# A four-layer graph attention kernel: what is loaded first, and when the later layers' weights and the second batch's adjacency follow

## The chip, the cores and the metric

The kernel runs on one core of one Trainium2 chip. The core has a matrix engine (PE; its weight loads are listed as PEld), a vector engine (DVE), a scalar engine (ACT), a general engine (POOL, GpSimd), a queue engine (SP), and 16 DMA engines [...]. The metric is the device time of one execution in microseconds (us), as the median of repeated runs. Before the change it is 3160.04 us (3 runs, 3157.3 to 3164.76).

## What is computed

16 graphs ("batches") of 1024 nodes with 256 features each, and one 1024 x 1024 adjacency of 0 and 1 per graph. Four attention layers follow one another; each normalizes the features, clamps them at zero, attends over the neighbours and adds the result to the features. Cut to what matters:

```python
# x: (16, 1024, 256) float32, adj: (16, 1024, 1024) int32
h = maximum(layernorm(x), 0); x = x + L0(h, adj, W, a)   # softmax over neighbours of leaky_relu(f1_i + f2_j)
h = maximum(layernorm(x), 0); x = x + L1(h, adj, W, a)   # exp(-leaky_relu(...)), then elu
h = maximum(layernorm(x), 0); x = x + L2(h, adj, W, a)   # softmax of relu(...), then elu
h = maximum(layernorm(x), 0); x = x + L3(h, adj, ...)    # 4 heads of 64, leaky_relu 0.01, bias, relu, layernorm
# each of L0, L1, L2:
#   Wh = h @ W;  e_ij = act(Wh_i @ a[:256] + Wh_j @ a[256:]);  e_ij masked by adj
#   out_i = sum_j softmax_j(e_ij) Wh_j
```

## The kernel before

The kernel is written as Python generators that are traced into one program. Two streams of batches (even ones and odd ones) are interleaved; each `yield t` advances its stream's counter by `t`, and the stream whose counter is lower is traced next. The order of tracing is the program order. A scheduler then places each engine's instructions by that order, but lets an instruction that it takes to be ready early float ahead; `tc.keep_in_program_order(i)` pins `i` behind whatever was traced before it on the same engine.

The loads of one batch, and the test of its adjacency (which looks for values other than 0 and 1):

```python
    def load(b):
        narrow = narrows[b % 2]                       # adjacency as bytes, in DRAM
        ...
        for c in range(NI // 2):                      # NI = 8: four casts int32 -> uint8, DRAM to DRAM
            cast = nc.gpsimd.dma_start(rows[c], adj[b, ts(c, 2 * P), :]...)
            tc.keep_in_program_order(cast)
        yield
        mask = masks[b] = nodes.tile([P, NI // 2, N, 2], U8, name="mask")
        for c in range(NI // 2):                      # four transposing loads
            turn = nc.sync.dma_start_transpose(mask[:, c]..., narrow[:, ts(c, P)])
            if b > 1:
                tc.keep_in_program_order(turn)
            yield
        xs[b] = nodes.tile([P, NI, D], F32, name="x_b")
        queue = nc.gpsimd if b > 1 else nc.sync
        queue.dma_start(xs[b]..., in_blocks(x[b]))    # 1 MB of features
        yield

    def test(b):
        for i in range(NI):
            adj_i = adjs.tile([P, N], BF, name="adj_i")          # 4 buffers
            nc.gpsimd.dma_start(adj_i, adj[b, ts(i, P), :])
            square = nc.scalar.activation(adj_i, adj_i, AF.Square, ..., accum_out=squares[:, b, i : i + 1])
            tc.keep_in_program_order(square)
            yield
```

`prepare()` loads the layers' weights `W[l]` and vectors `a`, and makes from them a few extra columns of each `W[l]` (W times a), so that a projection gives the attention scores too:

```python
    def prepare():
        ...
        scratch = [edges.tile([P, N], F32, name="weights0") for _ in EXT]
        def extend(l): ...                            # 3 small DVE multiplies into W[l][:, :, D:]
        def fetch(l): ...                             # on SP: W[l], a; for l = 3 also bias, gamma, beta
        fetch(0)
        for l in range(3):
            if l == 0:
                yield
            fetch(l + 1)
            for k in range(NK):
                for s in range(2):
                    nc.vector.tensor_tensor_reduce(prod, W[l][:, k, :D], scratch[l][:, ts(s, D)], ...)   # L200
            extend(l)
            yield
        for s in range(2):
            for k in range(NK):
                nc.vector.tensor_mul(prod, W[3][:, k, :D], scratch[3][:, ts(s, D)])                      # L209
                nc.vector.tensor_reduce(wa[:, k, 3:, s], ...)                                            # L210
        extend(3)
        ...                                           # norms of the columns, by PE and DVE, into a flag
        yield
```

One batch projects its features for layer 0 (four pairs of node blocks), and then attends in each layer. `weigh` makes the eight 128 x 1024 tiles of edge weights on DVE (L292) from a row of scores in PSUM, of which there is one for both streams; while they come, the products of the first two node blocks run (L380); then those of the other six, and behind each pair of blocks the projection for the next layer (L271):

```python
        def attend(l, V, finish, then):
            behind = weigh(b, ...)
            yield from start(behind, b)
            ...
            for j in range(NI):
                next(behind)                          # DVE: weights of block j
                product(0, j)                         # PE
                product(1, j)
                yield 0.9
            for i in range(NI):
                if i > 1:
                    for j in range(NI): product(i, j)
                finish(i, accs.pop(i))                # frees the accumulator, adds into x_b
                if l == 2:
                    next(testing)
                if i != 0:
                    yield 3.6
                if i % 2 == 1:
                    yield from steps
                    steps = project(b, then, xb, i // 2, following[1])    # yields 0.5, 1.0, 2.5
                yield from islice(steps, 1)
            yield 1.0
            yield from steps
        ...
        if b == 0:
            for _ in chain(preparing, loading):       # all other weights, columns and loads of batch 0
                pass
        V = yield from attend(0, V, finish0, 1)
        next(coming, None)                            # coming = load(b + 2): its casts
        V = yield from attend(1, V, finish, 2)
        V3 = yield from attend(2, V, finish, 3)
        # then layer 3, four heads in eight half-heads of 8 x 0.9 + 0.5 + 0.5, the rest of `coming` among them
```

And the two streams:

```python
    LAG = 120.0
    def stream(first):
        if first:
            for _ in load(first):
                yield 2.0
        for b in range(first, B, 2):
            yield from batch(b)

    loading, preparing = load(0), prepare()
    for _ in islice(loading, 2 + NI // 2):
        pass
    next(preparing)
    streams = [[0.0, stream(0)], [LAG, stream(1)]]
```

## Time and profile before

| | before |
|---|---|
| time, median of 3 | 3160.04 us |
| span of the profiled execution | 3156.4 us |
| PE busy | 3003.8 us (95%) |
| DVE busy | 2376.8 us (75%) |
| POOL busy | 1078.1 us (34%) |
| ACT busy | 729.5 us (23%) |
| PE busy in the first 40 us | 17.6 us |
| PE busy from 400 to 3000 us | 2529.8 us of 2600 |
| PE busy from 3000 us to the end | 113.4 us of 156 |

A page of the profile has the busy time of each engine, the span in slices, the chain of waits that ended last, and groups of instructions by line of the kernel. A line of the timeline reads: start, duration, engine, source line, operation, what it writes and reads, how many; in brackets, how long the engine stood idle ahead of it and what ended that. In a table of windows, each row is a stretch of time with the busy time and, in brackets, the number of instructions of each engine, then the granted clock of PE (1.00 is full), the mean busy share of the 16 DMA engines (overlapping packets can bring it over 1) and the rate in GB/s.

### The profile page before, as it was taken

How to read it: one execution, taken by the hardware profiler on the slowest of the kernel's cores; microseconds unless marked ns; L12 is line 12 of the kernel's file. 1: busy time of each engine (PE TensorE's matmuls, PEld its weight loads, DVE VectorE, ACT ScalarE, POOL GpSimd, SP SyncE). 2: the span in 40 equal slices, each digit the busy share in tenths (PEclk: the TensorE clock that was granted, in tenths of full speed). 3: DMA queues.
4: the chain of work that ended last, by engine and by line, in shares of the span. 5: the costliest groups of instructions: out<-in, count | busy, mean ns of one | idle time of the engine just before them, and what ended most of it. 6: DMA issues, size and time to landing. Idle time of an engine off the chain costs nothing.

```text
span 3156.4 us, 35596 instructions
## 1 busy us (share of the span) xinstructions
PE 3003.8 (95%) x12678; PEld 2065.5 (65%) x12678; DVE 2376.8 (75%) x5243; ACT 729.5 (23%) x1729; POOL 1078.1 (34%) x1396
## 2 busy tenths in 40 slices
PE   7899999999999999999999999999999999999986
PEld 5675766668666686666767567575776757766652
DVE  5677778786878768887687876878768787787756
ACT  1221223123131221312213122131222213222130
POOL 1323325233252432423325233342324333243232
PEclk9999999999999999999999999999999999999998
DMA  5512212022120221302302122022121121001010
GB/s 112 62 19 27 47 21 50 18 27 53 15 60 7 54 30 11 67 1 54 41 8 60 14 47 34 14 54 27 40 27 22 46 27 44 11 14 27 1 27 15
DMA packets 116872, 105.53 MB, mean 33 GB/s; under 512 B 73680, under 2 KB 91216, under 8 KB 116688
## 3 DMA queue, kind: packets, MB, share of 16 engines
q0 software_dynamic: 44256, 81.80, 15.9%
q1 hardware_dynamic: 72432, 21.37, 3.6%
q8 instruction: 103, 1.69, 0.2%
q14 instruction: 81, 0.66, 0.1%
HBM read 153.49 MB, written 33.55 MB: 59 GB/s over the span
## 4 chain that ended last, share of the span: by engine, by line
PE 67%; DVE 21%; POOL 6%; ACT 2%; issue 2%; DMA 1%; ACTq 0%; SPq 0%; POOLq 0%; DVEq 0%
PE acc L380 32%; PE acc L487 19%; PE acc L271 11%; DVE weights L292 9%; PE misc L264 2%; POOL rstd L239 2%; DVE stats L251 2%; PE row L288 2%; DVE above L317 1%; DVE centered L256 1%; POOL y L447 1%; DVE above L318 1%; ACT below L315 1%; POOL x_b L319 1%; DVE y L448 1%
## 5 line engine op out<-in xcount | busy, mean ns | idle before, releaser
L380 PE MATMUL acc<-V,weights 128*128 128x257 f32 x6144 | 1439.9, 384 | 24.1 <-DVE weights L292 11.0
L380 PEld LDWEIGHTS acc<-V,weights 128*128 128x128 f32 x6144 | 1148.0, 191 | 336.0 <-DVE weights L292 83.8
L487 PE MATMUL acc<-weights,V 128*65 128x512 f32 x2048 | 960.1, 592 | 2.0 <-DVE weights L292 1.7
L292 DVE SCALAR_TENSOR_TENSOR weights<-row,ex,mask 128x1024 f32<-128x1024 f32 x512 | 626.7, 1274 | 12.6 <-PE row L288 9.1
L271 PE MATMUL acc<-W,hT 128*128 128x259 f32 (+1 forms) x2048 | 532.7, 399 | 55.5 <-DVE above L317 24.5
L239 POOL TENSOR_TENSOR rstd<-rstd,minus_half 128x2 f32<-128x2 f32 (+1 forms) x320 | 302.7, 949 | 701.9 <-DVE rstd L238 687.2
L271 PEld LDWEIGHTS acc<-W,hT 128*128 128x128 f32 x2048 | 386.3, 195 | 192.4 <-issue 68.9
L292 DVE SCALAR_TENSOR_TENSOR weights<-row,V,mask 128x1024 f32<-128x1024 f32 x384 | 475.5, 1273 | 46.9 <-PE row L288 46.9
L487 PEld LDWEIGHTS acc<-weights,V 128*65 128x65 f32 x2048 | 272.3, 138 | 351.3 <-issue 307.4
L319 POOL TENSOR_TENSOR x_b<-x_b,above 128x256 f32<-128x256 f32 x256 | 193.4, 758 | 687.8 <-DVE above L318 621.9
L315 ACT ACTIVATE below<-acc,inv 128x256 f32<-128x256 f32 x256 | 120.7, 474 | 827.6 <-DVE inv L308 532.6
L251 DVE BATCH_NORM_STATS2 stats<-x_b 128x6 f32<-128x256 f32 x512 | 208.5, 415 | 110.2 <-POOL x_b L319 102.0
L266 ACT COPY hT<-misc 128x512 f32<-128x512 f32 x256 | 149.3, 584 | 442.7 <-PE misc L264 442.5
L447 POOL TENSOR_TENSOR y<-y,bias 128x512 f32<-128x512 f32 x64 | 82.0, 1281 | 388.9 <-DVE y L505 345.2
L256 DVE TENSOR_SCALAR centered<-x_b,mv 128x256 f32<-128x256 f32 x512 | 209.4, 411 | 4.7
L264 PEld LDWEIGHTS misc<-ident,centered 128*128 128x128 f32 x1024 | 127.2, 142 | 110.0 <-issue 44.8
L264 PE MATMUL misc<-ident,centered 128*128 128x128 f32 x1024 | 164.6, 277 | 36.3 <-DVE centered L256 27.7
L333 ACT ACTIVATE V<-acc,rstd 128x3 f32<-128x3 f32 x384 | 98.9, 262 | 417.5 <-PE acc L271 416.6
L337 DVE TENSOR_SCALAR V<-acc,rstd,V 128x256 f32<-128x256 f32 x256 | 133.1, 538 | 67.0 <-ACT V L333 65.5
L317 DVE TENSOR_SCALAR above<-acc,inv 128x256 f32<-128x256 f32 x256 | 122.2, 480 | 68.0 <-ACT below L315 66.9
L497 ACT COPY sums<-acc 65x512 f32<-65x512 f32 x128 | 74.4, 581 | 353.2 <-PE acc L487 353.1
L132 ACT ACTIVATE adj_i<-adj_i,minus_half 128x1024 bf16<-128x1024 bf16 x128 | 145.8, 1139 | 0.0
(68 smaller groups left out, 1890.5 us busy)
## 6 DMA issues: line engine op xcount, KB each, us to landing
adj_i<-in_adj_dram POOLq DMA_DIRECT2D x128, 256.0 KB, 3.9
narrow<-in_adj_dram POOLq DMA_DIRECT2D x64, 256.0 KB, 9.0
out_dram<-y POOLq DMA_DIRECT2D x32, 512.0 KB, 4.0
x_b<-in_x_dram POOLq DMA_DIRECT2D x14, 1024.0 KB, 6.7
x_b<-in_x_dram SPq DMA_DIRECT2D x2, 1024.0 KB, 7.3
mask<-narrow SPq DMA_TRANSPOSE x64, 3.8
W<-in_L_gnn_W_dram SPq DMA_DIRECT2D x3, 256.0 KB, 11.4
weights<-in_L_gnn_a_dram SPq DMA_DIRECT2D x3, 256.0 KB, 12.7
```

Source lines behind the costliest of these rows:

```text
L239: nc.gpsimd.tensor_tensor(r, r, minus_half.to_broadcast([P, n]), op=ALU.pow)
L251: nc.vector.bn_stats(stats, xb[:, 2 * pair + n, :])
L256: nc.vector.tensor_scalar(centered[:, n, :], xb[:, 2 * pair + n, :], mv[:, n, 0:1], 0.0, op0=ALU.subtract, op1=ALU.max,)
L264: nc.tensor.transpose(turned[:, k, ts(n, P)], centered[:, n, ts(k, P)], ident)
L266: nc.scalar.copy(hT, turned)
L271: nc.tensor.matmul(projected, hT[:, k, ts(n, P)], W[l][:, k, :], start=(k == 0), stop=(k == NK - 1),)
L292: nc.vector.scalar_tensor_tensor(w, r, c(j), masks[b][:, j // 2, :, j % 2], op0=op, op1=ALU.mult)
L315: nc.scalar.activation(below, acc[:, :D], AF.Exp, scale=inv)
L317: nc.vector.tensor_scalar(above, acc[:, :D], inv, 0.0, op0=ALU.mult, op1=ALU.max)
L319: nc.gpsimd.tensor_add(xi, xi, above)
L380: nc.tensor.matmul(accs[i], weights[j][:, ts(i, P)], V[:, j, : D + 1], start=(j == 0), stop=(j == NI - 1),)
L487: nc.tensor.matmul(accT, V3[:, j, h, :], weights[h * NI + j][:, ts(g, HALF)], start=(j == 0), stop=(j == NI - 1),)
```

## The change

Batch 0 is to get at first only what it needs: its casts, its features, layer 0's weights and its masks. The weights of each later layer are fetched, and its extra columns made, one layer ahead of their use and pinned there in program order; the columns are made right behind the last weights tile of the layer before, the small multiplies of `extend` for layers 1 to 3 by GpSimd instead of DVE. Batch 1's casts and features follow the columns of layer 1. The test of batch 0's adjacency no longer fetches ahead. The features of batches from 2 on are pinned in program order too. `scratch` uses the other stream's weights buffers.

```diff
--- before.py
+++ after.py
@@ -96,6 +96,13 @@
     xs, masks = {}, {}
     narrows = [dram.tile([N, N // 2], BF, name=f"narrow{n}") for n in range(2)]
 
+    def fetch_nodes(b: int):
+        xs[b] = nodes.tile([P, NI, D], F32, name="x_b")
+        queue = nc.gpsimd if b > 1 else nc.sync
+        fetch = queue.dma_start(xs[b].rearrange("p (c t) f -> p c t f", t=2), in_blocks(x[b]))
+        if b > 0:
+            tc.keep_in_program_order(fetch)
+
     def load(b: int):
 
 
@@ -106,6 +113,8 @@
                 rows[c], adj[b, ts(c, 2 * P), :].rearrange("(q t) j -> q t j", t=2)
             )
             tc.keep_in_program_order(cast)
+        if b < 2:
+            fetch_nodes(b)
         yield
 
         mask = masks[b] = nodes.tile([P, NI // 2, N, 2], U8, name="mask")
@@ -113,20 +122,20 @@
             turn = nc.sync.dma_start_transpose(
                 mask[:, c].rearrange("p n t -> p (n t)").bitcast(BF), narrow[:, ts(c, P)]
             )
-            if b > 1:
-                tc.keep_in_program_order(turn)
+            tc.keep_in_program_order(turn)
             yield
-        xs[b] = nodes.tile([P, NI, D], F32, name="x_b")
-        queue = nc.gpsimd if b > 1 else nc.sync
-        queue.dma_start(xs[b].rearrange("p (c t) f -> p c t f", t=2), in_blocks(x[b]))
-        yield
+        if b > 1:
+            fetch_nodes(b)
+            yield
 
     def test(b: int):
 
         for i in range(NI):
 
             adj_i = adjs.tile([P, N], BF, name="adj_i")
-            nc.gpsimd.dma_start(adj_i, adj[b, ts(i, P), :])
+            fetch = nc.gpsimd.dma_start(adj_i, adj[b, ts(i, P), :])
+            if b == 0:
+                tc.keep_in_program_order(fetch)
 
 
             square = nc.scalar.activation(
@@ -149,6 +158,7 @@
     beta = const.tile([P, D], F32, name="beta")
 
     def prepare():
+
 
 
         forms = [
@@ -157,62 +167,70 @@
             (0.0, 1.0, -1.0),
             (L3_SLOPE, 1 - L3_SLOPE, L3_SLOPE - 1),
         ]
-        scratch = [edges.tile([P, N], F32, name="weights0") for _ in EXT]
+        scratch = [edges.tile([P, N], F32, name="weights1") for _ in EXT]
 
         def extend(l: int):
             n = EXT[l] // 3
+            engine = nc.vector if l == 0 else nc.gpsimd
             for c, factor in enumerate(forms[l]):
-                nc.vector.tensor_scalar_mul(
+                engine.tensor_scalar_mul(
                     W[l][:, :, D + c * n : D + (c + 1) * n],
                     wa[:, :, l : l + n, 0 if c == 2 else 1],
                     factor,
                 )
 
         def fetch(l: int):
+            def begin(dst: bass.AP, src: bass.AP):
+                fetched = nc.sync.dma_start(dst, src)
+                if l > 0:
+                    tc.keep_in_program_order(fetched)
+
             if l < 3:
-                nc.sync.dma_start(
-                    W[l][:, :, :D], ins[f"L{l}_W"].rearrange("(k p) o -> p k o", p=P)
-                )
-                nc.sync.dma_start(scratch[l][:, : 2 * D], on_all_partitions(ins[f"L{l}_a"], 2 * D))
+                begin(W[l][:, :, :D], ins[f"L{l}_W"].rearrange("(k p) o -> p k o", p=P))
+                begin(scratch[l][:, : 2 * D], on_all_partitions(ins[f"L{l}_a"], 2 * D))
                 return
             for k in range(NK):
-                nc.sync.dma_start(
+                begin(
                     W[3][:, k, :D].rearrange("p (h e) -> p h e", h=H),
                     ins["L3_W"][:, ts(k, P), :].rearrange("h p e -> p h e"),
                 )
             for s, name in enumerate(("L3_a_src", "L3_a_dst")):
                 first = ins[name]
-                nc.sync.dma_start(
+                begin(
                     scratch[3][:, ts(s, D)].rearrange("p (h e) -> p h e", h=H),
                     bass.AP(tensor=first.tensor, offset=first.offset, ap=[[0, P], [T * E, H], [1, E]]),
                 )
             for t, a in ((bias, ins["L3_bias"]), (gamma, ins["L3_gamma"]), (beta, ins["L3_beta"])):
-                nc.sync.dma_start(t, on_all_partitions(a, D))
-
-        fetch(0)
+                begin(t, on_all_partitions(a, D))
+
         for l in range(3):
-            if l == 0:
-                yield
-            fetch(l + 1)
+            fetch(l)
+            yield
             for k in range(NK):
                 for s in range(2):
                     prod = work.tile([P, D], F32, name="above", bufs=2)
-                    nc.vector.tensor_tensor_reduce(
+                    made = nc.vector.tensor_tensor_reduce(
                         prod, W[l][:, k, :D], scratch[l][:, ts(s, D)], op0=ALU.mult, op1=ALU.add,
                         scale=1.0, scalar=0.0, accum_out=wa[:, k, l, s : s + 1],
                     )
+                    if l > 0:
+                        tc.keep_in_program_order(made)
             extend(l)
             yield
+        fetch(3)
+        yield
         for s in range(2):
             for k in range(NK):
                 prod = work.tile([P, D], F32, name="above", bufs=2)
-                nc.vector.tensor_mul(prod, W[3][:, k, :D], scratch[3][:, ts(s, D)])
+                tc.keep_in_program_order(
+                    nc.vector.tensor_mul(prod, W[3][:, k, :D], scratch[3][:, ts(s, D)])
+                )
                 nc.vector.tensor_reduce(
                     wa[:, k, 3:, s], prod.rearrange("p (h e) -> p h e", h=H), AX.X, ALU.add
                 )
         extend(3)
 
-        nc.vector.tensor_scalar_add(beta, beta, -2.0)
+        tc.keep_in_program_order(nc.vector.tensor_scalar_add(beta, beta, -2.0))
 
         groups = (3 + H) * 2
         wa2 = small.tile([P, NK, groups], F32, name="wa2", bufs=1)
@@ -387,6 +405,13 @@
                 next(behind)
                 product(0, j)
                 product(1, j)
+                if b == 0 and j == NI - 1:
+
+
+                    next(preparing)
+                    if l == 0:
+                        next(loading[1])
+                    next(preparing, None)
                 yield 0.9
             for _ in behind:
                 pass
@@ -427,8 +452,7 @@
         for steps in pairs:
             yield from steps
         if b == 0:
-            for _ in chain(preparing, loading):
-                pass
+            next(preparing)
         V = yield from attend(0, V, finish0, 1)
         next(coming, None)
         V = yield from attend(1, V, finish, 2)
@@ -523,16 +547,13 @@
 
 
     def stream(first: int):
-        if first:
-            for _ in load(first):
-                yield 2.0
+        for _ in loading[first]:
+            yield 2.0
         for b in range(first, B, 2):
             yield from batch(b)
 
-    loading, preparing = load(0), prepare()
-
-    for _ in islice(loading, 2 + NI // 2):
-        pass
+    loading, preparing = [load(0), load(1)], prepare()
+    next(loading[0])
     next(preparing)
     streams = [[0.0, stream(0)], [LAG, stream(1)]]
     while streams:
```

## Prediction

> **What bounds the kernel now.** I first read the page's totals: PE is busy 3003.8 of 3156.4 us, so the whole change plays in the 153 us that PE is not busy. The table of windows says where these lie: 22.4 us in the first 40 us, 70 us in the 2600 us from 400 to 3000, and 42.6 us in the last 156 us.
>
> ```profile
> 5.00:10.00 5.00, 1.09 (x4) 0.72 (x4) 1.79 (x8) 0.27 (x1) 0.97 (x2) 1.00 0.98 235
> 25.00:30.00 5.00, 2.50 (x12) 1.89 (x10) 0.00 (x0) 1.01 (x3) 0.00 (x0) 0.84 1.09 314
> 60.00:80.00 20.00, 19.43 (x96) 16.26 (x94) 9.55 (x31) 2.79 (x8) 2.44 (x4) 1.00 0.00 1
> ```
>
> The last two columns are the DMA share and GB/s: at the start the DMA engines are full and PE (the second number) is idle; 40 us later PE is full and nothing is moved. Next, the chain that ended last, in order of time, for the start:
>
> ```profile
> 1.40 6.73 DMA W<-in_L_gnn_W_dram
> 8.14 23.66 DMA weights<-in_L_gnn_a_src_dram
> 31.82 0.42 DVE above L209
> ```
>
> The end waits for a vector of layer 3 that nothing needs before 150 us. The timeline shows how it gets there: SP hands it out and is held for 10 us by the full DMA engines, the masks of batch 0 stand behind it on SP, and DVE has the product with it (L209) ahead of the last V blocks of batch 0.
>
> ```profile
> 8.14 10.13 SPq L185 DMA_DIRECT2D weights<-in_L_gnn_a_src_dram  x1
> 29.32 10.36 SPq L113 DMA_TRANSPOSE mask<-narrow  x4
> 31.82 0.42 DVE L209 TENSOR_TENSOR above<-W,weights 128x256 f32<-128x256 f32 x1 [7.55 <-DMA weights<-in_L_gnn_a_src_dram]
> 38.28 1.28 DVE L292 SCALAR_TENSOR_TENSOR weights<-row,V,mask 128x1024 f32<-128x1024 f32 x1
> ```
>
> So the first weights tile starts at 38.28 us. Last, the later windows: one stream runs alone until about 146 us and again from about 3000 us. Alone, the end of a layer leaves PE without work; with two streams a little is lost where a batch begins:
>
> ```profile
> 3005.07 1.11 PE L271 MATMUL acc<-W,hT 128*128 128x259 f32 x4 [2.62 <-DVE above L317]
> 3010.30 0.69 PE L264 MATMUL misc<-ident,centered 128*128 128x128 f32 x2 [3.29 <-DVE centered L256]
> ```
> ```profile
> 320.00:340.00 20.00, 16.66 (x84) 13.36 (x83) 14.18 (x35) 7.50 (x22) 8.61 (x9) 1.00 0.33 106
> 540.00:560.00 20.00, 17.32 (x68) 13.71 (x67) 12.26 (x34) 7.35 (x20) 14.05 (x21) 0.83 0.46 132
> 600.00:620.00 20.00, 20.00 (x76) 11.99 (x75) 17.02 (x31) 2.32 (x5) 2.81 (x3) 1.00 0.00 0
> ```
>
> [...] with SP and GpSimd both issuing, the share is 1.11 from 10 to 32 us and every transfer is late (a_src took 23.7 us to land). What is taken out of either queue therefore helps the other. [...] So the casts keep their queue, and what the change can do is to put less in front of them and beside them. [...] 0.50 from 30 to 36 us and from 130 to 138 us, where PE had waited. Fewer holes bring some clock too; I count nothing for it.
>
> **Part 1: the start.** Two things must be there for the first weights tile. The masks: batch 1's four casts, which run alone, took 11.2 us from their first issue (127.30) until SP went on to the transposes (138.5; DMA share 1.1 in between), and the transposes land in a median of 5.7 us. In front of them go 1 MB of features (3.5 us at the 298 GB/s seen from 6 to 7 us) and layer 0's W and a (0.5 MB, 1.7 us). GpSimd begins the casts at about 1.6 us instead of 2.47, as no adj_i is fetched ahead. 1.6 + 11.2 + 3.5 + 1.7 = 18; a first transpose lands at about 24. The row of scores: layer 0's a arrives at about 10.5 us as now (it is already third on SP), its columns take 1.5 us, pair 0's projection starts at about 14 as now. The other three pairs followed with stalls (DVE waited 2.5 us for layer 2's a, 7.55 for a_src); a pair without them costs about 2.9 us (2.0 us for its 8 matmuls, and the wait for the two accumulators to be emptied by ACT 0.26 and DVE 0.54). 14 + 3 x 2.9 = 22.7 for the last pair's start. From there to the first weights tile took 5.4 us (32.86 to 38.28) at half clock; I take 4. First tile at about 26.5: **-12 us**. DVE, PE and DMA arrive close together, so no single one is left to gain from.
>
> **Part 2: columns that come back on the path.** Four L200 take 1.4 us (11.02 to 12.4). They now stand on DVE between the last weights tile of layer 0 and the `finish` that frees the accumulator. There DVE had 0.8 us idle (L307 at 48.90 waited that long for PE). So +0.6 us, and again in layer 1. Layer 3's (four L209 and L210, 0.76 us each, and the norms) take 3.5 us behind layer 2's tiles, with 1.4 us idle there (142.82): +2. About **+3 us**. The small multiplies of `extend` go to GpSimd, idle then for tens of us; their result is needed only 8 us later: nothing.
>
> **Part 3: the streams move closer.** A batch's own steps are 16 (projection), 3 x 49.4 (8 x 0.9 + 7 x 3.6 + 4 x 4 + 1) and 70.6 (layer 3), in all 235. Before, batch 0 began at step 0 and batch 1 at 120 + 6 x 2 = 132. Now stream 0 spends 8 steps on its transposes, and batch 1 has its first load step taken from it: 120 + 4 x 2 = 128. The distance falls from 132 to 120. Following the yields by hand to the end, one stream is alone at the tail from step 116 of batch 15 on, where it was 99.5. So 12 steps at the head and 16 at the tail move from alone to shared. Shared, 1776 steps of each stream took 2854 us, 0.80 us per step of one stream. Alone, the 16 steps at the tail are the stretch from 3000.7 to 3017.7, 17 us with the two long waits shown, against 13 shared; the 12 at the head are about 133 to 147, 14 us against 10. **-7 us**, rounded down.
>
> **Part 4: the test of batch 0.** Each adj_i is now issued right behind the x_b addition of its own node block, and the ACT square behind it must wait for the transfer (3.7 to 6.3 us to land in that stretch). ACT also copies hT and empties accumulators, so PE can be held. The scheduler puts what it takes to be ready ahead of the square, and the accumulators are double. **+2 us**, a guess within 0 to 6.
>
> **Part 5: the shared part.** With distance 132, a batch of stream 0 began 12 steps before the other's layer-2 tiles, and then both wanted the one row of scores (it waited 2.5 steps in the yields); a batch of stream 1 began 17 steps behind them. The windows show about 4.4 us lost at the first kind (320 to 360) and 3.4 at the second (540 to 580). With 120 both begin 2 to 5 steps behind the start of the other's layer-2 tiles, and no two rows collide. For it: the end of layer 1, the stretch with the long waits, then lies beside the other stream's layer 3, which has matmuls without end. Against it: a projection (12 us of DVE) and eight tiles (9.6 us) fall on DVE together. I take 0.3 us less for each of 14 boundaries: **-4 us**, give or take 10.
>
> Features from batch 2 on are issued in the middle of layer 3, some 50 us before use, and land in 6.7 us: nothing. Sum: -12 + 3 - 7 + 2 - 4 = -18, so 3160 - 18 = 3142 us.
>
> **The rivals.** *Nothing but the start*: the streams' distance does not matter because PE is full anyhow; then -12 + 3 + 2, 3153 us. For it speaks that 600 to 620 shows PE at 20.00 of 20. *The new phase hurts*: the collision of projection and tiles on DVE costs 2 us more at each of 14 boundaries, +28 in place of -4: 3174 us. For it, DVE is at 4.00 of 4 us between 336 and 344 even now; against it, PE has products of the other stream in hand soon after. *Masks become the wait*: casts and transposes take the place of a_src and the first tile starts only at 31 us: 3147. Against it, casts alone took 11.2 us. *The phase helps more*: half of the 8 us per pair of batches goes: 3125.
>
> **Range and chances.** The start is sure to 3 us, the columns and the test to 4 together, the alone stretches to 3, the shared part to 10, which sets the range: 3122 to 3160 us. 2% is 63 us, more than the whole start takes: faster by over 2% has 0.02, slower by over 2% 0.02 (a bad phase of over 4 us per boundary), within 2% 0.96.
>
> **What would show it.** First L292 at 25 to 28.5 us; no DVE wait for a vector of layers 1 to 3 before it; the first output leaving about 20 us earlier than at 329.6; outputs of successive batches about 195 us apart, where they alternated between 165 and about 217; PE idle from 3000 us to the end down by 4 us or more; ACT waiting for adj_i DMA around 115 to 175 us. The prediction would be wrong if PE's idle time between 400 and 3000 us moved by more than 10 us from 70, or if the first tile waits for masks past 30 us.

## The result, and the profile after

The changed kernel takes 3114.47 us (median of 5 runs, 3112.5 to 3116.73) where the one before, on the same chip, takes 3157.74 us (5 runs, 3150.46 to 3164.76): a ratio of 0.9862, 95% interval 0.9846 to 0.9877. It is 43 us faster. The prediction was 3142 us with a range from 3122 to 3160: right in sign, too small by more than half, and the result lies below the range.

The start came nearly as predicted. This is the chain that ended last, for the first 27 us of the changed kernel (start, duration, what). No vector of layer 3 is left in it; what is waited for is layer 0's own `a`, then its columns (L212), the four projections (L289), and the first weights tile (now L310) at 24.76 us, where it was 38.28.

```profile
1.92 7.95 DMA weights<-in_L_gnn_a_dram
9.91 0.10 issue
10.01 0.42 DVE above L212
...
21.94 2.04 PE acc L289 x8
24.00 0.27 ACT V L351
24.33 0.43 issue
24.76 2.25 DVE weights L310 x2
```

In the timeline of SP, the fetch of a_src that held SP for 10.13 us holds it for 2.81 us, and comes behind the masks:

```profile
22.52 1.32 SPq L122 DMA_TRANSPOSE mask<-narrow  x1
...
28.75 2.81 SPq L184 DMA_DIRECT2D weights<-in_L_gnn_a_src_dram  x1
```

The windows of the changed kernel, for the stretches that the prediction shows of the kernel before (start and end, length, busy time of PE, PEld, DVE, ACT and POOL, then clock, DMA share and GB/s; the batch boundary that lay at 540 now lies at 520):

```profile
25.00:30.00 5.00, 3.74 (x14) 2.34 (x15) 5.00 (x5) 0.00 (x0) 0.00 (x0) 1.00 0.86 198
60.00:80.00 20.00, 17.32 (x74) 12.13 (x73) 15.44 (x28) 2.03 (x6) 3.37 (x5) 1.00 0.59 53
320.00:340.00 20.00, 17.98 (x81) 13.21 (x80) 17.28 (x44) 7.87 (x18) 11.79 (x14) 1.00 0.34 79
520.00:540.00 20.00, 18.19 (x86) 14.61 (x87) 16.41 (x40) 9.09 (x21) 13.76 (x21) 1.00 0.48 106
600.00:620.00 20.00, 20.00 (x76) 11.14 (x75) 19.36 (x25) 2.76 (x7) 1.41 (x2) 1.00 0.00 1
```

PE has more work at 25 us (3.74 against 2.50), less at 60 (17.32 against 19.43), and no less than before in the middle, and the clock is 1.00 at both boundaries (it was 0.83 at 540). But a gain at the start does not explain 43 us, and these windows do not say how much work got done in them. The milestones do. The trace gives for each kernel the time of the first weights tile of batch 0 and of batch 1, of the first output, from there to the output of batch 14 (seven pairs of batches with both streams at work), and from that to the last output (one stream alone). The kernels of the experiments are in the same table; "time" is the median in us; the milestones come from one profiled execution of each kernel, which was up to 4.9 us longer than the median (testfree; both: 3.7), so a few us between rows mean little. From output 15 to the end it is another 10.5 us, but 14.1 in nearsp and nearspin and 12.7 in busy.

| kernel | time | first tile | tile of batch 1 | output 0 | outputs 0 to 14 | outputs 14 to 15 |
|---|---|---|---|---|---|---|
| before | 3157.7 | 38.3 | 175.8 | 329.6 | 2677.2 | 139.2 |
| after | 3114.5 | 24.8 | 154.7 | 331.1 | 2653.2 | 117.2 |
| far132 | 3153.2 | 24.6 | 169.0 | 326.5 | 2673.3 | 141.5 |
| near120 | 3130.3 | 40.3 | 162.5 | 336.7 | 2663.6 | 118.6 |
| xpin | 3153.3 | 37.7 | 173.5 | 327.2 | 2672.6 | 140.9 |
| near120x | 3115.8 | 37.6 | 159.8 | 334.1 | 2652.1 | 118.6 |
| testfree | 3111.8 | 25.9 | 155.9 | 330.3 | 2653.2 | 120.9 |
| cols3 | 3117.8 | 24.8 | 159.7 | 336.1 | 2654.8 | 116.9 |
| both | 3109.9 | 25.5 | 155.4 | 329.6 | 2653.2 | 118.6 |
| farboth | 3145.9 | 25.0 | 168.9 | 322.3 | 2674.3 | 139.2 |
| split | 3105.3 | 25.3 | 148.8 | 323.0 | 2653.0 | 118.6 |
| nearsp | 3133.2 | 38.0 | 160.2 | 334.5 | 2667.0 | 118.6 |
| nearspin | 3133.2 | 38.8 | 160.9 | 335.2 | 2666.2 | 118.7 |
| busy | 3118.7 | 38.5 | 160.8 | 335.1 | 2652.9 | 118.6 |
| tiny | 3117.1 | 38.8 | 159.5 | 333.7 | 2652.0 | 118.6 |
| split112 | 3110.7 | 25.6 | 142.1 | 325.2 | 2656.8 | 116.8 |
| split85 | 3176.1 | 25.2 | 138.0 | 332.2 | 2730.5 | 101.0 |

The first two rows hold the surprise: the tile that is 13.5 us earlier leaves the first output 1.5 us *later*; 24.0 us are won with both streams at work, and 22.0 at the tail. So the questions are: what made the middle and the tail shorter, and where did the start's gain go?

### The profile page after: what moved, and what is told of

It reads as the page before. It is cut to its first block, busy times and chain, and to the rows that moved or that the text cites. A ratio compares the mean times of both kernels' runs of the same rounds, so it can differ in the third digit from the quotient of the medians.

```text
span 3112.0 us, 35525 instructions
## 1 busy us (share of the span) xinstructions
PE 2981.7 (96%) x12678; PEld 2047.5 (66%) x12678; DVE 2337.8 (75%) x5234; ACT 737.1 (24%) x1729; POOL 1081.2 (35%) x1405
## 4 chain that ended last, share of the span: by engine, by line
PE 78%; DVE 15%; POOL 3%; ACT 2%; issue 1%; DMA 1%; SPq 0%; ACTq 0%; POOLq 0%; DVEq 0%
PE acc L398 35%; PE acc L511 25%; PE acc L289 11%; DVE weights L310 8%; PE misc L282 3%; PE row L306 2%; ACT adj_i L141 1%; PE misc L526 1%; POOL y L471 1%; POOL rstd L257 1%; DVE V L355 1%; DVE stats L269 1%; POOL x_b L337 1%; DVE centered L274 1%; ACT below L333 1%
## 5 line engine op out<-in xcount | busy, mean ns | idle before, releaser
L398 PEld LDWEIGHTS acc<-V,weights 128*128 128x128 f32 x6144 | 1141.6, 190 | 348.6 <-DVE weights L310 100.6
L310 DVE SCALAR_TENSOR_TENSOR weights<-row,ex,mask 128x1024 f32<-128x1024 f32 x512 | 627.8, 1274 | 6.1 <-PE row L306 5.6
L289 PE MATMUL acc<-W,hT 128*128 128x259 f32 (+1 forms) x2048 | 515.4, 389 | 26.0 <-ACT hT L284 14.8
L310 DVE SCALAR_TENSOR_TENSOR weights<-row,V,mask 128x1024 f32<-128x1024 f32 x384 | 482.0, 1274 | 46.6 <-PE row L306 46.6
L289 PEld LDWEIGHTS acc<-W,hT 128*128 128x128 f32 x2048 | 379.2, 191 | 138.4 <-ACT hT L284 38.2
L274 DVE TENSOR_SCALAR centered<-x_b,mv 128x256 f32<-128x256 f32 x512 | 192.6, 384 | 15.7 <-PE misc L282 12.2
L355 DVE TENSOR_SCALAR V<-acc,rstd,V 128x256 f32<-128x256 f32 x256 | 133.4, 538 | 37.7 <-ACT V L351 34.9
L141 ACT ACTIVATE adj_i<-adj_i,minus_half 128x1024 bf16<-128x1024 bf16 x128 | 145.8, 1139 | 20.0 <-DMA adj_i<-in_adj_dram 20.0
```

Source lines behind the costliest of these rows:

```text
L141: square = nc.scalar.activation(adj_i, adj_i, AF.Square, bias=minus_half, accum_out=squares[:, b, i : i + 1])
L274: nc.vector.tensor_scalar(centered[:, n, :], xb[:, 2 * pair + n, :], mv[:, n, 0:1], 0.0, op0=ALU.subtract, op1=ALU.max,)
L289: nc.tensor.matmul(projected, hT[:, k, ts(n, P)], W[l][:, k, :], start=(k == 0), stop=(k == NK - 1),)
L310: nc.vector.scalar_tensor_tensor(w, r, c(j), masks[b][:, j // 2, :, j % 2], op0=op, op1=ALU.mult)
L355: nc.vector.tensor_scalar(V[:, i, :D], projected[:, :D], rstd, V[:, i, D : D + 1], op0=ALU.mult, op1=ALU.mult,)
L398: nc.tensor.matmul(accs[i], weights[j][:, ts(i, P)], V[:, j, : D + 1], start=(j == 0), stop=(j == NI - 1),)
```

## The experiments

Theory: the distance of the streams (120 steps where it was 132) makes nearly all of the time, and the order of loads next to nothing. Rival: the order of loads makes it, and the distance is a by-product.

**The distance alone, both ways.** far132 is the changed kernel with the distance put back; near120 is the kernel before with the distance shortened (its stream 1 still loads for 12 steps, hence 108 + 12).

```diff
# far132, on the changed kernel
-    LAG = 120.0
+    LAG = 132.0
# near120, on the kernel before
-    LAG = 120.0
+    LAG = 108.0
```

> The changed kernel with LAG 132 in place of 120, so that batch 1 again begins 132 steps behind batch 0; everything else stays. Theory P (the distance between the streams made the shared part cheaper): outputs alternate between about 163 and 220 us again, the tail behind the next-to-last output is about 139 us, and the time is about 3145 us, only the 13 us of the start below the kernel before. Rival X (the pinned fetch of the features, or another of the pins, did it): outputs stay about 190 us apart and the time is about 3120 us.

> The kernel before with LAG 108 in place of 120, so that batch 1 begins 120 steps behind batch 0; nothing else. Theory P: outputs about 190 us apart, tail about 117 us, first weights tile still at 38 us, time about 3128 us (the changed kernel plus its 13.5 us of start). Rival X: the shared part stays at 382.5 us per pair of batches; only less time alone, about 3150 us.

far132 took 3153.16 us, 0.9987 of before (0.998 to 0.9994); near120 3130.34, 0.991 (0.9894 to 0.9927). All of the new order of loads at the old distance is worth 4 us, where its expectation had 13; the distance alone is worth 27. Outputs come 163 and 220 us apart in turn in far132, as before, and 193 and 188 in near120. The yields say why: at 132, a stream's start meets the other on the row of scores and waits, and the starts settle at 100.6 and 139.0 steps apart; at 120 they stay at 116.8 and 118. So in the last batch 99.5 steps are done beside other work before, and 115.8 after.

What the even phase saves in the middle is seen in the windows around an odd output (544.65 in the kernel before, 530.03 in near120), first of the kernel before, with the wait of PE in it, then of near120:

```profile
549.56 2.13 PE L271 MATMUL acc<-W,hT 128*128 128x268 f32 x4 [2.60 <-DVE above L317]
548.00:552.00 4.00, 2.44 (x6) 1.93 (x7) 2.24 (x8) 2.90 (x8) 3.95 (x8) 0.58 0.80 249
552.00:556.00 4.00, 4.00 (x13) 3.07 (x13) 1.51 (x4) 1.10 (x4) 2.50 (x5) 0.57 1.00 229
556.00:560.00 4.00, 4.00 (x19) 3.29 (x18) 1.32 (x3) 0.89 (x3) 0.00 (x0) 1.00 0.02 4
```
```profile
529.00:533.00 4.00, 4.00 (x22) 3.52 (x21) 2.80 (x5) 1.98 (x6) 3.68 (x6) 1.00 0.37 135
533.00:537.00 4.00, 2.36 (x13) 1.29 (x12) 3.92 (x16) 1.83 (x4) 3.73 (x7) 1.00 0.95 212
537.00:541.00 4.00, 4.00 (x21) 3.44 (x20) 2.17 (x9) 1.94 (x4) 2.99 (x5) 1.00 1.00 265
```

Before, PE has one hole of 2.60 us, and then the clock is at half: PE reads as busy from 552 to 556, but makes 13 matmuls where the next 4 us hold 19. In near120 two holes of 0.66 and 0.98 us stand in place of the one, and the clock stays at 1.00. The clock's record has five half-clock stretches between 300 and 2990 us before, 23.9 us in all; near120 and the changed kernel have one of 3.4 us each (at 2817 and at 2983).

**The pinned features alone.** xpin is the kernel before with the fetches of features from batch 2 on kept in their place of the program; near120x is near120 with the same edit.

```diff
+        fetch = queue.dma_start(xs[b]..., in_blocks(x[b]))
+        if b > 1:
+            tc.keep_in_program_order(fetch)
```

> The kernel before, with only the fetch of the features from batch 2 on pinned in program order (in the middle of layer 3 instead of behind the output). Theory P: the fetch was never waited for, so 3158 us within 4, outputs alternating as before. Rival X: the fetch behind the output stood in GpSimd's way at the batch's end, so the shared part falls to about 379 us per pair, about 3134 us.

> The kernel before with both LAG 108 and the pinned features, so everything of the change but the start. If the two are worth what they were alone, 3130 - 4 = 3126 us. If the fetch behind the output stands in the way of the even phase more than of the uneven one (a hole of 1.1 us 8 us behind each even output, which the changed kernel does not have): 3120 us, and the start is worth only 6 us of the changed kernel's 43.

xpin took 3153.25 us, 0.9986 (0.998 to 0.9993); near120x 3115.78, 0.986 (0.9843 to 0.9876). At the old distance the pin is worth 4 us, at the new one 15, more than either expectation for near120x. These two edits, a number and a pin, bring near120x to within 1.3 us of the whole change, although its first tile comes at 37.6 us and not at 24.8. By far132 and xpin, which take the same time, the earlier start, with its columns and its test, is worth nothing at the old distance either.

**Where the start's gain goes.** From the first tile to the first output near120x takes 296.5 us (334.1 - 37.6), the changed kernel 306.3; PE is idle for 12.7 us of it in the one and for 21.3 in the other. The timeline of the changed kernel, PE and DVE, has two holes in that stretch. The first is layer 3's columns: four products (L226, L228) and the norms (L237) in one piece on DVE, and PE waits 2.77 us in its order for the norms' matmul (L240):

```profile
129.40 0.41 DVE L226 TENSOR_TENSOR above<-W,weights 128x256 f32<-128x256 f32 x1
...
133.41 0.20 DVE L237 TENSOR_TENSOR wa<-wa 128x28 f32<-128x28 f32 x1
...
133.66 0.62 PE L240 MATMUL misc<-wa,ones 128*128 128x14 f32 x4 [2.77 <-DVE wa L237]
```

The second is the test of batch 0, whose squares on ACT (L141) wait for adj_i; the copy of hT behind them is late, and PE waits 2.73 us for it:

```profile
141.96 1.15 ACT L141 ACTIVATE adj_i<-adj_i,minus_half 128x1024 bf16<-128x1024 bf16 x1 [1.24 <-DMA adj_i<-in_adj_dram]
...
143.46 1.06 ACT L284 COPY hT<-misc 128x512 f32<-128x512 f32 x2
...
144.09 2.02 PE L289 MATMUL acc<-W,hT 128*128 128x259 f32 x8 [2.73 <-ACT hT L284]
```

testfree takes the pin off the fetches of this test. cols3 moves layer 3's columns to an earlier place, behind the fifth node block of layer 1. both is cols3 with three adj_i fetched ahead at that place. farboth is both at the old distance.

```diff
# testfree, on the changed kernel
-            if b == 0:
-                tc.keep_in_program_order(fetch)
# cols3, on the changed kernel
-                if b == 0 and j == NI - 1:
+                if b == 0 and l < 2 and j == NI - 1:
...
+                if b == 0 and l == 1 and i == 4:
+                    next(preparing)
# both, on cols3; test(0) fetches tiles 0 to 2 first, then i + 3 ahead of square i
                     next(preparing)
+                    next(testing)
# farboth, on both
-    LAG = 120.0
+    LAG = 132.0
```

> The changed kernel with the fetches of batch 0's adjacency test left free to float, as before. Theory T (ACT's 20 us of waiting for adj_i hold PE in batch 0's layer 2, one hole of 2.7 us among it): 3 to 5 us faster, about 3110 us, first weights tile about 1 us later. Rival: PE has the other stream's products and loses nothing, and four fetches in front delay the start by 2 us: about 3116 us.

> The changed kernel with layer 3's columns made in the middle of layer 1's attention of batch 0 (behind its fifth node block) and not behind layer 2's weights tiles. Theory S (the start's 13 us are lost again around 120 to 200 us, in holes of PE and the half clock that follows them, where batch 0's layer 2 has the columns on DVE and the adj_i waits on ACT): the hole of 2.8 us ahead of the norms' matmul goes, 3 to 5 us faster, about 3110 us. Rival R (the start is lost to the shared part's order, whatever stands in those holes): no change within 2 us.

> As cols3, and the adjacency test of batch 0 gets its first three tiles in the middle of layer 1's attention and each further one three blocks ahead, all pinned. Theory S: ACT no longer waits for adj_i and the hole of 2.7 us goes too: another 3 us, about 3107 us, without the 1 us later first tile of the free test. Rival R: 3112 to 3114 us.

> As both, with LAG 132. Theory S: what far132 lost between 119 and 200 us comes back in good part: first output about 319 us in place of 326.5, time about 3146 us. Rival R: first output at 326, time 3152 us.

testfree took 3111.77 us, 0.9853 (0.9837 to 0.987), cols3 3117.79, 0.9866 (0.985 to 0.9883), both 3109.91, 0.9843 (0.9827 to 0.986), farboth 3145.9, 0.9957 (0.994 to 0.9974). cols3 was a miss: moved in one piece, the columns only stand ahead of layer 2's first tile, which comes at 126.0 us where it came at 119.9, and PE loses its time there instead (from 120 to 126 us it is busy for 4.82 us at a clock of 0.72, in the changed kernel for 5.61 at 1.00). The waits for adj_i are worth 6 to 8 us beside cols3; testfree is 2.7 us faster in the median, but its runs (3111.4 to 3116.63) overlap with the changed kernel's. farboth is 36 us slower than both: that confirms the distance a second time.

So split spreads the same four products, one behind each of the node blocks 2 to 5 of layer 1, and puts the norms last of all:

```diff
# split, on both
-        extend(3)
-        tc.keep_in_program_order(nc.vector.tensor_scalar_add(beta, beta, -2.0))
+                if (s, k) == (1, NK - 1):
+                    extend(3)
+                    tc.keep_in_program_order(nc.vector.tensor_scalar_add(beta, beta, -2.0))
+                yield
...
-                if b == 0 and l == 1 and i == 4:
+                if b == 0 and l == 1 and 2 <= i < 6:
                     next(preparing)
-                    next(testing)
+                    if i == 4:
+                        next(testing)
...
+    for _ in preparing:                               # the norms, behind all batches
+        pass
```

> The kernel 'both' (layer 3's columns under node block 4 of layer 1, three adj tiles of batch 0's test fetched ahead), with layer 3's four column products spread, one behind each of the node blocks 2 to 5 of layer 1 in batch 0, and the norms' matmul placed last. Theory (after the change the gain of the start is given back between 120 and 202 us because 3.5 us of column work in one piece stands on DVE in the path, in 'both' before attend-2's first tile, 127.4 us): that tile comes at 121 to 124 us, the first output 5 to 8 us earlier than in 'both' (322 to 325), 3102 to 3105 us. Rival (the place does not matter, PE's idle time there comes from the half clock and from batch 1's start alone): first output at 328 to 330, 3109 to 3112 us.

split took 3105.26 us, 0.9832 (0.9815 to 0.9848), the fastest of all. Its timeline has layer 2's first tile at

```profile
120.81 6.05 DVE L322 SCALAR_TENSOR_TENSOR weights<-row,V,mask 128x1024 f32<-128x1024 f32 x5 [1.91 <-PE row L318]
```

where both has

```profile
127.42 9.63 DVE L321 SCALAR_TENSOR_TENSOR weights<-row,V,mask 128x1024 f32<-128x1024 f32 x8 [1.65 <-PE row L317]
```

and the first output at 323.0 instead of 329.6. The medians differ by 4.7 us and the intervals of the two ratios overlap; the 6.6 us are read from the two traces, where all later milestones are equal. Which share is the spreading and which the later norms was not told apart. From the first tile to the first output split takes 297.8 us, 8.5 less than the changed kernel and about what near120x takes, and PE is idle for 13.8 us of it. This is where the start's gain had gone.

**Why the features' pin is worth 15 us.** Seen in the timeline of near120: the unpinned fetch is issued by GpSimd 2.8 us after the even outputs, among the additions to x_b, and a `centered` on DVE there takes 1.27 us; some 5 us later PE stands idle for 1.14 us. First theory: the issue of 0.77 us holds GpSimd. Rival: the transfer of 1 MB disturbs the additions. nearsp gives the fetch of near120 to SP; nearspin gives that of near120x to SP. busy is near120x with a second write of the whole output, 1 MB, from SP at the moment of the output; tiny writes only 4 KB there. Both extra writes go to a scratch area and change nothing else.

```diff
# nearsp and nearspin
-        queue = nc.gpsimd if b > 1 else nc.sync
+        queue = nc.sync
# busy, on near120x
+        nc.sync.dma_start(in_blocks(again), y.rearrange("p (c t) h e -> p c t (h e)", t=2))
# tiny, on near120x
+        nc.sync.dma_start(again[:P, :8], y[:, NI - 1, 0, :8])
```

> The kernel before with the distance 120 (near120, 3130 us), and the features of every batch fetched from SP's queue in place of GpSimd's from batch 2 on, free to move as before. Theory (the features' fetch costs time because its issue, about 0.8 us, holds GpSimd, which has half of the x_b additions at the end of a batch): taken off GpSimd the hole of 1.1 us of PE some 8 us after the even outputs is gone, and the time is that of near120x, 3114 to 3119 us. Rival 1 (the transfer of 1 MB itself disturbs what runs then): no change, 3128 to 3132 us. Rival 2 (what counts is when the buffer of x_b and the masks are filled): in between, 3120 to 3127 us.

> The fourth corner of queue and place of the features' fetch at distance 120. On GpSimd and free to move it made 3130 us, on GpSimd and kept in its place of the program (about 55 us before the output) 3116, on SP and free 3133. Here it is on SP and kept in that place. Theory (the place alone counts: a fetch at the batch's end meets the additions and normalisations there): 3113 to 3118 us, no hole of 1.1 us of PE behind the even outputs, about 379 us per pair of batches. Rival (the queue counts too, SP's issues of this fetch stand before something that is needed): 3122 to 3133 us.

> The kernel near120x (distance 120, features fetched by GpSimd in their place of the program, 3116 us), with a second write of the whole 1 MB output y to a scratch area in DRAM, started by SP at the moment of the output. It adds only DMA traffic at the place where the unpinned features' fetch ran; GpSimd and DVE have the same work as in near120x. Theory (traffic in flight beside the additions and normalisations costs the 1.6 to 2 us per pair of batches, whoever starts it): the hole of 1.1 us of PE some 6 to 8 us after the even outputs is back and a centered of over 1.2 us in it, 3126 to 3134 us. Rival (traffic does not matter; the order of things on the queues or some tens of ns of timing decide): 3114 to 3119 us.

> Control of the run before: near120x with a second write of only 8 of y's numbers per partition (4 KB) started by SP at the moment of the output. Traffic theory: no hole, 3114 to 3118 us. Rival (the slow centered is a matter of some tens of ns, which any further wait or instruction at that place can tip): the hole may be there too, 3126 to 3134 us.

nearsp took 3133.15 us, 0.9921 (0.9904 to 0.9937): the first theory fell. Of its 17 us above near120x, 3.6 stand behind the last output and nearly all of the rest in the middle. nearspin took 3133.22, 0.9913 (0.9895 to 0.9931), and it did not test what it was meant to: on SP the pinned fetch still went out at the moment of the output, since a pin only holds it behind SP's own earlier work, and there was none. busy took 3118.69, 0.9873 (0.9856 to 0.9891), tiny 3117.11, 0.9871 (0.9854 to 0.9889); the hole of near120 is gone in tiny, and in busy it is left behind one of the seven even outputs. In busy's windows, behind another of these outputs, the DMA engines are full beside the additions, and PE loses nothing, so the rival fell too:

```profile
717.00:719.00 2.00, 2.00 (x11) 1.76 (x10) 1.96 (x6) 0.85 (x4) 1.62 (x3) 1.00 1.10 352
719.00:721.00 2.00, 2.00 (x10) 1.46 (x8) 1.98 (x11) 0.35 (x1) 1.53 (x3) 1.00 1.01 244
```

What is left is seen when the timelines of near120x and of nearsp are laid side by side, in the same place after the same output. near120x:

```profile
715.91 0.54 POOL L131 DMA_DIRECT2D adj_i<-in_adj_dram  x1 [0.37 <-ACT V L335]
715.95 0.35 DVE L258 TENSOR_SCALAR centered<-x_b,mv 128x256 f32<-128x256 f32 x1
716.22 0.99 DVE L339 TENSOR_SCALAR V<-acc,rstd,V 128x256 f32<-128x256 f32 x2
716.47 0.74 POOL L321 TENSOR_TENSOR x_b<-x_b,above 128x256 f32<-128x256 f32 x1
```

nearsp:

```profile
717.35 0.55 POOL L129 DMA_DIRECT2D adj_i<-in_adj_dram  x1 [0.32 <-ACT V L333]
717.42 1.39 DVE L256 TENSOR_SCALAR centered<-x_b,mv 128x256 f32<-128x256 f32 x1
717.90 0.74 POOL L319 TENSOR_TENSOR x_b<-x_b,above 128x256 f32<-128x256 f32 x1
...
721.62 0.87 PE L264 MATMUL misc<-ident,centered 128*128 128x128 f32 x6 [1.07 <-DVE centered L256]
```

The same GpSimd work stands in the same order. `centered` begins 0.04 us behind GpSimd's issue in the one and 0.07 in the other, and in the other it ends only at 718.81, 0.17 us after GpSimd's addition; everything behind it on DVE is late, and PE waits 1.07 us. In near120 it ends 0.15 us after the addition as well. In nearsp it is recorded 0.48 us ahead of the addition and takes 1.39 us for 0.35; GpSimd's issue begins ahead of `centered` in both. The traces of the kernel before and of the changed one show the same end elsewhere: each of the 116 `centered` of more than 0.45 us ends 0.15 to 0.16 us behind an addition or multiplication of GpSimd. Another 173 lie across one and take 0.45 us or less, so lying across one is not enough. That the one instruction holds the other up is the author's reading; no run shows how.

The traces say how often this happens. Behind each of the seven even outputs, 3.2 us later, near120, nearsp and nearspin have a `centered` of 1.27 to 1.40 us; near120x and tiny have none, busy and the changed kernel have one. The pair of batches with it takes 379.7 us in the changed kernel, where the pairs on both sides of it take 378.7. By that a slow `centered` costs 1.0 us, an estimate of 7 of the 11.5 us that the pin is worth in the middle. So, by this estimate, more than half of the gain goes with where DVE's and GpSimd's instructions fall against each other at the end of a batch. Neither the issue nor the transfer alone sets it; what exactly tips it, and what makes the other 4 to 5 us, stays open. So do the 4 us of xpin: it has as many slow `centered` as the kernel before (14, at other places).

**Is shorter always better?**

```diff
# split85 and split112, on split
-    LAG = 120.0
+    LAG = 85.0        # and 112.0
```

> As split, with the distance of the streams set 35 steps shorter (LAG 85 in place of 120). Theory (the distance sets the time by two things, how long one stream runs alone at head and tail, and whether starts of a batch fall on the other's rows of scores): the yields then give starts about 150 and 89 steps apart, uneven like before, so the shared part is that of the uneven phase (about 382 us per pair of batches, +3 each, +20) and the tail alone is 12 to 25 us shorter than split's: 3095 to 3125, with outputs unevenly apart. Rival (only the length of the alone stretches counts): 3080 to 3092 us.

> split (3105 us) with the distance 8 steps shorter, 112. By the yields the starts then settle to the same 117/118 steps apart, as a stream that comes too early waits for the row of scores, so the shared part and the tail stay (379 us per pair, about 118 us between the last two outputs); only batch 1 starts 8 steps earlier at the head, where each step alone costs 0.3 us more than shared. Theory (pattern and length alone): first output 0 to 3 us later, last output 1 to 4 us earlier than split's, 3101 to 3105 us. Rival (the exact distance matters to the shared part): outputs no longer 187/191 apart, over 3110 us.

split85 took 3176.11 us, 1.0061 (1.0044 to 1.0078): its tail is 17.6 us shorter than split's, but with outputs 157 and 233 us apart the middle is 77.5 us longer (390 us per pair where split has 379), far beyond both expectations. PE has holes of 2.5 to 3.9 us around every output. From output 0 to output 14 it is idle for 101.7 us where split has 64.3, and 88.7 us run at half clock where split has none; the two together are worth up to 82 us, an estimate from these numbers (37.4, and half of 88.7). split112 took 3110.73, 0.9849 (0.9831 to 0.9866), slower than its theory and where its rival put it, though the outputs keep 188 and 192 us between them: batch 1 starts 6.7 us earlier than in split, but the first output comes 2.2 us later and the middle takes 3.8 us more. So the pattern of starts decides the large amounts, and where exactly the streams meet still moves a few us.

## Why the prediction was wrong

The largest misses are three: the features' pin, put at nothing; Part 5, a guess from PE's idle time alone; and Part 3, mis-sized. In the terms of the prediction, from the traces of the kernel before, of near120, of near120x and of the changed kernel:

| term | predicted | measured |
|---|---|---|
| Part 1, first tile | -12 | -13.5 |
| Parts 2 and 4, columns and test, up to the first output | +5 | +9.8 |
| Part 3, from alone to shared | -7 | -15.5 |
| Part 5, the shared part | -4 | -13.6 |
| the features' pin, in the shared part | 0 | -11.5 |
| sum | -18 | -44.3 |

The two executions differ by 44.4 us, the medians by 43.3.

**Part 1 (the start, -12): right.** The first tile moved from 38.28 to 24.76 us, -13.5; the last pair's projection started at 21.94 where 22.7 was worked out. That the casts keep GpSimd's queue was assumed; no run moved them.

**Part 2 and Part 4 (columns +3, test +2): right in kind, too small.** From the first tile to the first output the changed kernel takes 9.8 us more than near120x, which has neither; split gets 8.5 of it back. In Part 2, "Layer 3's (four L209 and L210, 0.76 us each, and the norms) take 3.5 us ... +2" counted DVE's time, and missed PE's wait for the norms' matmul and the waits on DVE behind it: by the traces of both and split, spreading the columns and moving the norms to the end is worth 6.6. For the test, testfree does not contradict the "guess within 0 to 6"; the squares did wait for adj_i, 20.0 us in all by the group of L141. There was a sign of this in the reading: the three stretches of PE's idle time that the prediction lists make 135 of its 153 us, and nearly all of the rest lies between 40 and 400 us, where the start's gain went. With Part 1 all this makes the start worth about 1 us in the end, by the medians of near120x and the changed kernel.

**Part 3 (-7): right mechanism, short by about 8.** The steps do move from alone to shared, and outputs came 191 and 188 us apart, near the 195 written. But "Alone, the 16 steps at the tail are ... 17 us" came from one stretch of the profile; near120's tail is 20.6 us shorter, and has 330 matmuls where the kernel before has 382. The working also forgot its own consequence at the head: 12 steps of stream 0 that are now shared take 12 x 1.6 = 19 us instead of 14, so the first output had to come later by 5 us. near120 shows 7.2, of which 2.1 stand already in its first tile. The net of the 5.1 and the 20.6 is 15.5. The expectation of a first output 20 us earlier contradicted Part 3.

**Part 5 (-4): the step that failed.** "I take 0.3 us less for each of 14 boundaries" was a guess at PE's idle time. From output 0 to output 14 near120 makes as many matmuls as the kernel before (11064 and 11066) in 13.6 us less. PE's idle time explains little of it: within a pair of batches it falls from 10.8 to 10.0 us in most pairs, but not in the first and the last, and from 74.9 to 73.2 us over all seven. The larger term is what the prediction put in so many words at nothing: "Fewer holes bring some clock too; I count nothing for it" (the clock that it reads at 0.50 from 30 to 36 us is PE's). In that stretch the clock is at half for 24.5 us before and for 3.4 us in near120, and 21 us fewer are up to 10.5 us of PE work, an estimate from the recorded clock of 0.50 (in the kernel before, eight matmuls of L271 take 3.66 us at 551.69, at half clock, and 2.02 at 556.42, at full). 1.7 + 10.5 = 12.2 of the 13.6.

**"Features from batch 2 on ... nothing": the second step that failed.** As they come early enough either way, the prediction put them at nothing, without asking what the fetch of the kernel before runs into. At the new distance the pin is worth 11.5 us between outputs 0 and 14. This is PE's idle time, which falls from 73.2 to 62.0 us, and not the clock (3.4 us at half in both). Another 2.7 us stand in the first tile. The pin also takes batch 2's features out of the crowded start, where near120 fetched them at 17.8 us; that this is the reason is not shown, as the first tiles of near120x, busy and tiny, whose start is the same, lie 1.2 us apart.

**The rivals.** "The phase helps more" came nearest, and was still given too little; by its own terms (4 us for each of seven pairs in place of Part 5's 4 in all) it would have come to 3118, not 3125. "Nothing but the start" had it the wrong way round: without the distance the change is worth 4 us. "The new phase hurts" did not come; split85 shows that a phase can. And the criterion "PE's idle time between 400 and 3000 us moved by more than 10 us from 70" did not tell: it went from 70.2 to 65.2 us, because a fixed window holds more work in the faster kernel, and because matmuls at half clock count as busy (4.00 of 4 us from 552 to 556, at 0.57). PE's idle time from 3000 us to the end fell from 42.6 to 31.9, as predicted by "4 or more", but there the changed kernel has 112 us left and the one before 156; from output 14 to the end it fell from 40.3 to 33.0.

## What to carry to other kernels

Where two streams share an engine that is 95% busy, ask first of a change in program order what it does to their distance: put the old distance back, and set the new one alone in the old kernel, before any part of the change is given credit. Count such gains per pair of batches, with the granted clock beside the busy share, and not as idle time in a fixed window. Work that moves from the start to a later place may have to be spread behind work of the other engines; in one piece it gave back here most of what it had saved.

## What was not expected of the hardware

- **A hole of 2.6 us can be enough for half clock, and one of 2.8 too little.** The kernel before has a hole of 2.6 us in PE behind each of its seven odd outputs; five brought half clock, those behind 1315 and 2080 us did not, and neither did the holes of 2.77 and 2.73 us in the changed kernel. The edges of the clock's records lie 3.41 us or a multiple of it apart in these traces, and what tells most of the holes apart is how much of one falls between two edges. The piece up to the edge at 548.64, where half clock begins, holds 1.76 us of idle PE; the piece up to 1316.63, in another of these holes, holds 1.65, and the clock stays:

```profile
545.23:548.64 3.41, 1.65 (x9) 0.95 (x7) 2.56 (x10) 0.78 (x3) 3.38 (x6) 1.00 0.73 277
548.64:552.05 3.41, 2.49 (x6) 1.96 (x7) 2.02 (x5) 2.72 (x8) 3.36 (x7) 0.50 0.79 232
1313.22:1316.63 3.41, 1.76 (x10) 1.06 (x8) 2.65 (x10) 0.80 (x4) 3.38 (x6) 1.00 0.70 267
1316.63:1320.04 3.41, 2.41 (x11) 2.06 (x12) 1.93 (x5) 3.18 (x9) 3.36 (x7) 1.00 0.76 227
```

  Cut at these edges, the 17 traces hold 15061 such pieces at full clock after the first 50 us. The 126 that were followed by half clock all had at least 1.41 us of idle PE, and none of the others had more than 1.75 (the kernel before and the changed one alone: 1777 pieces, 12 followed by half clock, 1.55 and 1.74 us).
- **The same DVE instruction can take four times as long.** `centered` (a 128x256 subtraction with a clamp, 0.35 us) took 1.27 to 1.40 us where it met GpSimd's issue of a DMA and its next addition. Over a whole kernel its mean is 411 ns in the kernel before and 384 in the changed one.
- **A fetch of 128 KB can hold SP for 10.13 us**, with the DMA engines' share at 1.08 in that time, and for 2.81 us at 0.94; everything behind it on SP waits, masks included (the first of them goes out at 29.32 us). What sets the length was not tested.
